# Two stacked transformers on one core: setup redone, buffer pools and the seam between the stacks rearranged

## The chip, the cores and the metric

The kernel runs on one core of a Trainium2 chip. The metric is the device time of one execution, in microseconds (us). "PE" is TensorE's matmul, "PEld" its weight load, DVE is VectorE, ACT is ScalarE, POOL is GpSimd, and SP is SyncE, which mostly issues DMAs. ACT and POOL issue DMAs too. Everything is float32.

## The reference

The input x has 2 sequences of 2048 tokens with 256 features. Six rows of conditioning (a shift, a gain and a gate for each of two stacks) come from c, one vector for each sequence.

```python
mod = (silu(c) @ wmod).reshape(2, 6, 1, 256)
sa, ca, ga, sb, cb, gb = (mod[:, i] for i in range(6))
ga, gb = away_from_zero(ga), away_from_zero(gb)       # |g| is at least 0.25
h = layernorm(x) * (1 + ca) + sa
x = x + ga * stack1(h)
h = layernorm(x) * (1 + cb) + sb
x = x + gb * stack2(h)

def stack1(out):                                       # 3 layers, 16 heads of 16
    for l in range(3):
        q, k, v = out @ Wq + bq, out @ Wk + bk, out @ Wv + bv
        Q, K = favor(q, omega), favor(k, omega)        # [exp(u - h), exp(-u - h)], u = q @ omega
        a = causal_linear_attention(Q, K, v)           # running sums of K v and of K
        h = layer_norm(out + a @ Wo + bo) * g1 + b1
        out = layer_norm(h + relu(h @ W1 + bf1) @ W2 + bf2) * g2 + b2
    return out

def stack2(x):                                         # 2 layers, 8 heads of 64
    for l in range(2):
        q, k, v = split(shift_token(x) @ wqkv)
        q, k = rotary_xpos(l2norm(q) * qs, l2norm(k) * ks)
        x = x + window_attention(q, k, v, 128) @ wo    # own and previous window of 128
        a, g = split((norm(shift_token(x)) * lg + lb) @ w1 + b1)   # 682 features each
        x = x + (a * gelu(g)) @ w2 + b2
    return x
```

## The kernel before

**Setup.** A pool `pro` holds what only the setup uses. `wmod` comes on two queues (L232), then all weights of the three layers of stack 1 on SP's queue (L251; the first Wq on ACT's). silu(c) is made by one ACT and three DVE operations (`sg`, L258 to L261). Twenty-four small matmuls make the six conditioning rows (`pm`, L300; `mod`, L307). Rows that must lie along the free axis on all 128 partitions (gains and biases of the norms) are kept in `brow`: `spread` widens columns on DVE (`wide`, L279), transposes them on PE (`rowtp`, L287) and copies them on ACT (L288). `omt` (L330 to L337) holds the matrices of the random features.

**Stack 1** works on 16 blocks of 256 tokens: 8 positions n of each sequence b. `favor_block(b, n)` loads x, normalizes (`normed`: statistics L354 and L355, `rs` L357 and L358, `dn` L361), turns to features on partitions (`turned`: four PE transposes `ntp` L371, ACT scale and shift L375), makes the residual on POOL (`scaled`: `res`, L382 to L385), and runs three layers, `favor_layer`. A layer: `pq` L414, `xs` L425, `pv` L430, the features `pu` L453 and `ft` L463, the running sum of K and its product with Q (`z`, POOL L484 and L485), `tk` L489, the scores `sc` L500 masked into `att` L506, `su` L520, the denominators `den` L548, the numerators `nd` L559 and L572, `po` L602, a norm, and the MLP (`pf` L624, `fr` on ACT L632, `acc` L635, the sum `s` L647), and a norm. A carried state `st` (L593) joins a block to the next of its sequence.

Four blocks are in work at once. `planned(jobs, 4)` lets each block run from one `yield` to the next and writes their steps into one order for PE by the times that the yields give: a step's own time, the time until its next can start, and a key ("attention", "mlp") that one block holds at a time. PE works this list in order. The other engines are ordered by a scheduler, and each works its own list in order too.

At the end of a block, `x1` = x + gate x output is written to DRAM (`xmid`, L685), normalized again, turned to `hm` and written to `hmid` (L690).

**Stack 2** loads the entry streams `s` from `hmid` (L724) with 16 loads at its start; a column between two 512-token streams is copied on POOL (L713), the first set to zero (L711), for the shift by one token. Each of its 2 layers has 32 attention tiles of 128 tokens and then an MLP over blocks of 512 tokens. The order on PE, DVE, ACT and POOL is written by hand: the table `WHEN` gives every step of a tile (names such as "q", "tp", "s0", "po") a time in units of one tile, about 14 us, and the steps of all tiles are sorted by tile number plus that time. A tile has `pqkv` L790 (q, k, v, a bank of PSUM each), cos and sin products (`qk` L802, `raw` L813, `rot` POOL L832, the sum L854), the l2 norm (`sq` L824, `ss` L842, L859), transposes `tp` L869, the copies `qT` and `kT`, `sim` L886, the softmax (`mx` L918, `ex` L926, `sum` L936, `pm` on POOL L941), transposes `ptp` L953 and copies `pT` L961, `av` L979, `po` L998, then the sum and norm of the MLP's entry (`mean` and `var` L1021). The MLP has `pg` and `pa` L1135, gelu L1143, the product L1144, `acc` L1173. A layer's MLP weights come by `load_mlp` and `load_w2`.

PSUM has 8 banks of 512 floats for each partition. Stack 1 divides them by tag: "mm" 3, "sc" 4, "acc" 1, in one pool. Stack 2 takes all 8 as one ring, `bank(name)`: each request gets the bank that was asked for longest ago, and waits until its last reader is done. SBUF is laid out by pools; where a pool is closed, what is opened later may lie on its place, and its first writer then waits for the last user of that place.

Of the kernel before, what the change touches and what calls it, by code (L numbers as in the profile page):

```python
# [8 lines left out]
F32 = mybir.dt.float32  # L9
# [5 lines left out]
P = 128  # L15
# [24 lines left out]
def block_kernel(ctx: ExitStack, tc: tile.TileContext, t: dict, out: bass.AP):  # L40
# [19 lines left out]
    nc.sync.dma_start(cst, t["consts"])  # L60
# [11 lines left out]
    mhalf = const.tile([P, 16], F32, name="mhalf")  # L72
    nc.gpsimd.memset(mhalf, -0.5)
    mod = const.tile([P, 6, KT, B], F32, name="mod")
    omt = const.tile([P, LA, 2, 4, 2, 8], F32, name="omt")
    bvb = const.tile([P, LA, D], F32, name="bvb")
    nc.gpsimd.dma_start(bvb, t["bv"].partition_broadcast(P))
# [54 lines left out]
    }  # L132
    FEED = 0.32
# [75 lines left out]
    attn_w, mlp_w = {}, {}  # L209


    with ExitStack() as c1:
        wp = c1.enter_context(tc.tile_pool(name="wA", bufs=1))
        psum = c1.enter_context(tc.tile_pool(name="psA", bufs=1, space=PSUM))
        brow = wp.tile([P, NROW, D], F32, name="brow")
        hp = c1.enter_context(tc.tile_pool(name="hA", bufs=3))
        work = c1.enter_context(tc.tile_pool(name="workA", bufs=2))

# [7 lines left out]
        def mm_tile(name):  # L226
            return psum.tile([P, TB], F32, tag="mm", name=name, bufs=3)

        with tc.tile_pool(name="pro", bufs=1) as pro:
            wmod = pro.tile([P, KT, 6 * D], F32, name="wmod")  # L230
            for kt in range(KT):
                (nc.scalar if kt else nc.sync).dma_start(wmod[:, kt, :], t["wmod"][kt * P : (kt + 1) * P, :])  # L232
            early = {b: load_x(b, 0) for b in range(B)}
            om_rep = pro.tile([P, LA, 8], F32, name="om_rep")
            for h in range(8):
                nc.gpsimd.dma_start(om_rep[16 * h : 16 * h + 16], t["omega"].rearrange("l d m -> d l m"))
            W = {}
            for l in range(LA):
                pool = shared if l < 2 else wp
                wa = pool.tile([P, ROOM], F32, tag=f"wa{l}", name=f"wa{l}")  # L240
                wb = pool.tile([P, ROOM], F32, tag=f"wb{l}", name=f"wb{l}")
                for room, at, name, kts, width in (
                    (wa, KT * DFF, "Wq", KT, D),
                    (wa, KT * DFF + KT * D, "Wk", KT, D),
                    (wb, NF * D, "Wv", KT, D),
                    (wb, NF * D + KT * D, "Wo", KT, D),
                    (wa, 0, "W1", KT, DFF),
                    (wb, 0, "W2", NF, D),
                ):
                    w = room[:, at : at + kts * width].rearrange("p (k n) -> p k n", k=kts)  # L250
                    (nc.scalar if (name, l) == ("Wq", 0) else nc.sync).dma_start(  # L251
                        w, t[name][l].rearrange("(k p) n -> p k n", p=P)
                    )
                    W[name, l] = w

            cv = vec[:, V_C : V_C + KT * B]
            sg = pro.tile([P, KT * B], F32, name="sg")
            nc.scalar.activation(sg, cv, AF.Exp, scale=-1.0)  # L258
            nc.vector.tensor_scalar(sg, sg, 1.0, None, ALU.add)
            nc.vector.reciprocal(sg, sg)  # L260
            nc.vector.tensor_tensor(sg, sg, cv, ALU.mult)  # L261

            cols = pro.tile([P, NROW, KT], F32, name="cols")

            def col(i, *parts):
                op = parts[2] if len(parts) > 2 else ALU.add
                if len(parts) == 1:
                    nc.vector.tensor_copy(cols[:, i, :], parts[0])
                else:
                    nc.vector.tensor_tensor(cols[:, i, :], parts[0], parts[1], op)  # L270

            def va(l, name):
                o = V_A + l * VA_N + VA[name]
                return vec[:, o : o + KT]

            def spread(lo, hi):
                for i in range(lo, hi, 2):
                    wide = pro.tile([P, 2 * KT, P], F32, tag="wide", name="wide", bufs=2)
                    nc.vector.tensor_copy(  # L279
                        wide,  # L280
                        cols[:, i : i + 2, :].rearrange("p a k -> p (a k)").unsqueeze(2).to_broadcast(
                            [P, 2 * KT, P]
                        ),
                    )
                    tp = mm_tile("rowtp").rearrange("p (a c) -> p a c", c=P)
                    for k in range(2 * KT):
                        nc.tensor.transpose(tp[:, k, :], wide[:, k, :], ident)  # L287
                    nc.scalar.copy(brow[:, i : i + 2, :].rearrange("p a (k c) -> p (a k) c", c=P), tp)  # L288

            for l in range(LA):  # L290
                col(R_G1 + l, va(l, "g1"))
                col(R_B1 + l, va(l, "b1"), va(l, "bf2"))
            for l in range(LA - 1):
                col(R_G2 + l, va(l, "g2"))
                col(R_B2 + l, va(l, "b2"), va(l + 1, "bo"))
            spread(0, R_G0)
            pm = mm_tile("pm")
            for m in range(6 * KT):
                for kt in range(KT):
                    nc.tensor.matmul(  # L300
                        pm[:, m * B : (m + 1) * B],
                        wmod[:, kt, m * P : (m + 1) * P],
                        sg[:, kt * B : (kt + 1) * B],
                        start=(kt == 0),
                        stop=(kt == KT - 1),
                    )
            nc.vector.tensor_copy(mod.rearrange("p a k b -> p (a k b)"), pm[:, : 6 * KT * B])  # L307
            for i in (1, 4):
                nc.vector.tensor_scalar(mod[:, i], mod[:, i], 1.0, None, ALU.add)
            for i in (2, 5):  # L310
                sgn = pro.tile([P, KT, B], F32, name=f"sgn{i}")
                nc.vector.tensor_scalar(sgn, mod[:, i], 0.0, 2.0, ALU.is_ge, ALU.mult)
                nc.vector.tensor_scalar(sgn, sgn, -1.0, None, ALU.add)
                neg = pro.tile([P, KT, B], F32, name=f"neg{i}")
# [4 lines left out]
            for b in range(B):  # L319
                col(R_G0 + b, mod[:, 1, :, b])  # L320
                col(R_B0 + b, mod[:, 0, :, b], va(0, "bo"))
                col(R_GE + b, va(LA - 1, "g2"), mod[:, 2, :, b], ALU.mult)
                col(R_BE + b, va(LA - 1, "b2"), mod[:, 2, :, b], ALU.mult)
            spread(R_G0, NROW)


            for hf in range(2):
                own, other = slice(64 * hf, 64 * hf + 64), slice(64 - 64 * hf, 128 - 64 * hf)
                for l in range(LA):
                    nc.vector.tensor_tensor(  # L330
                        omt[own, l, hf].rearrange("p h s m -> p (h s) m"),
                        om_rep[own, l, :].unsqueeze(1).to_broadcast([64, 8, 8]),
                        hm2[own, 8 * hf : 8 * hf + 8].unsqueeze(2).to_broadcast([64, 8, 8]),
                        ALU.mult,
                    )
                    nc.vector.tensor_scalar(omt[own, l, hf], omt[own, l, hf], 0.5, None, ALU.mult)
                    nc.vector.tensor_scalar(  # L337
                        omt[other, l, hf].rearrange("p h s m -> p (h s m)"),
                        nhalf[other, 64 - 64 * hf : 128 - 64 * hf],
                        0.25,  # L340
                        None,
                        ALU.mult,
                    )

        rp = c1.enter_context(tc.tile_pool(name="rA", bufs=2))
        fp = c1.enter_context(tc.tile_pool(name="featA", bufs=2))
        sp = c1.enter_context(tc.tile_pool(name="smallA", bufs=2))

        def normed(src):

            mv = sp.tile([P, NCA, 2], F32, tag="mv", name="mv")
            for c in range(NCA):
                bs = sp.tile([P, 6], F32, tag="bs", name="bs")
                nc.vector.bn_stats(bs, src[:, c, :])  # L354
                nc.vector.bn_aggr(mv[:, c, :], bs)  # L355
            rs = sp.tile([P, NCA], F32, tag="rs", name="rs")
            nc.scalar.activation(rs, mv[:, :, 1], AF.Ln, bias=eps_t)  # L357
            nc.scalar.activation(rs, rs, AF.Exp, scale=-0.5)  # L358
            dn = work.tile([P, NCA, D], F32, tag="dn", name="dn", bufs=3)
# [33 lines left out]
        nc.vector.tensor_reduce(par, hmask.rearrange("p (i q) -> p q i", q=2), AX.X, ALU.add)  # L393
# [5 lines left out]
        turn = [0]  # L399

        def favor_layer(b, n, l, h, hres):
# [45 lines left out]
            yield 5.2, 0.6, "attention"  # L447
            feat = []
# [44 lines left out]
            def scores(c):  # L493

                cs = slice(c * P, (c + 1) * P)
                scs = [psum.tile([P, KT, 2, P], F32, tag="sc", name="sc", bufs=4) for _ in range(4)]
# [121 lines left out]
            acc = psum.tile([P, NCA, D], F32, tag="acc", name="acc", bufs=1)  # L618
            fr = {}
            for f in range(NF + 1):  # L620
                if f < NF:
                    pf = psum.tile([P, TA], F32, tag="sc", name="pf", bufs=4)
# [8 lines left out]
                    fr[f] = fp.tile([P, TA], F32, tag="fr", name="fr", bufs=3)  # L631
# [16 lines left out]
            dn = normed(s)  # L648
# [9 lines left out]
        def next_weights():  # L658

            late.append(0)  # L660
            if len(late) == B:
                attn_w[0] = load_attn(0)
                mlp_w[0] = load_mlp(0)
# [663 lines left out]
```

## Time and profile before

| | |
|---|---|
| median of 3 runs | 3002.98 us (3001.48 to 3004.59) |
| profiled execution | 3000.0 us, span 2998.2 us |
| mean granted PE clock | 0.992 |
| PE | 2914.3 us busy (97% of the span), 19356 instructions |
| PEld | 2132.3 us (71%) |
| DVE | 1686.0 us (56%), 4194 instructions |
| ACT | 1344.5 us (45%), 3269 instructions |
| POOL | 1065.1 us (36%), 937 instructions |
| DMA | 57.10 MB, mean 19 GB/s |

The span is the profiled execution from its first to its last instruction, and the time of that execution has 1.8 us more. Busy times leave out the issuing of DMAs and waiting. In a chain of waits each line is a start, a length, and the work or wait that the next piece followed; "issue" is time in which the engine waited for nothing that the profile shows. PE's clock is the share of its full speed that the chip granted. A matmul shows as two records, a transpose as one.

### The profile page before, as it was taken

The page shows a single profiled execution, that of the slowest core. Times are in us where ns is not written, and L with a number is a line of the kernel's source. Part 1 is how long each engine was busy: PE and PEld are TensorE (multiplying, and loading weights), DVE is VectorE, ACT ScalarE, POOL GpSimd, SP SyncE. Part 2 cuts the span into 40 slices and gives each one's busy share as a digit, 9 for nine tenths or more (in the row PEclk, how much of TensorE's full clock was granted, in tenths as well). Part 3 has the DMA queues.
Part 4 walks back from the last instruction along what each step waited for, and adds up shares of the span by engine and source line. Part 5 has one row for each costly group of instructions (what it writes and reads, how often), then busy time and mean ns, then how long its engine had stood idle before and what let it go on. Part 6 is the DMA issues. An engine that isn't in the chain of part 4 may idle for free.

```text
span 2998.2 us, 49213 instructions
## 1 busy us (share of the span) xinstructions
PE 2914.3 (97%) x19356; PEld 2132.3 (71%) x19356; DVE 1686.0 (56%) x4194; ACT 1344.5 (45%) x3269; POOL 1065.1 (36%) x937
## 2 busy tenths in 40 slices
PE   6999999999999999999996999999999999999999
PEld 5888888888888888888873777776444777776444
DVE  5555565555565555655543777774224777775222
ACT  2333343334343334434333676665113766766211
POOL 2222233222332223322233666663002666664000
PEclk9999999999999999999997999999999999999999
DMA  5000010000100000001012000001000000000011
GB/s 184 1 1 1 1 36 22 1 1 1 36 22 1 1 1 29 29 1 43 15 42 77 1 1 1 1 1 58 0 0 10 20 1 1 2 1 8 28 43 35
DMA packets 37399, 57.10 MB, mean 19 GB/s; under 512 B 3720, under 2 KB 28720, under 8 KB 36656
## 3 DMA queue, kind: packets, MB, share of 16 engines
q1 hardware_dynamic: 36288, 52.37, 5.3%
q8 instruction: 153, 2.51, 0.3%
q0 software_dynamic: 464, 0.54, 0.1%
q10 hardware_dynamic: 416, 1.05, 0.1%
q14 instruction: 78, 0.64, 0.1%
HBM read 41.37 MB, written 12.58 MB: 18 GB/s over the span
## 4 chain that ended last, share of the span: by engine, by line
PE 88%; DVE 4%; ACT 3%; POOL 2%; DMA 1%; issue 1%; SPq 1%; DVEq 0%; ACTq 0%; POOLq 0%
PE acc L635 11%; PE pf L624 10%; PE pqkv L790 10%; PE pg L1135 5%; PE pq L414 5%; PE acc L1173 5%; PE pa L1135 4%; PE av L979 4%; PE sim L886 3%; PE ptp L953 3%; PE po L998 3%; PE sc L500 3%; PE nd L572 3%; PE pu L453 3%; PE pv L430 3%; PE po L602 3%
## 5 line engine op out<-in xcount | busy, mean ns | idle before, releaser
L635 PE MATMUL acc<-wb,fr 128*128 128x256 f32 x1536 | 397.3, 381 | 5.4 <-ACT fr L632 5.1
L624 PE MATMUL pf<-h,wa 128*128 128x256 f32 x1536 | 400.2, 384 | 1.1 <-ACT h L375 0.7
L632 ACT ACTIVATE fr<-pf,vec 128x256 f32<-128x256 f32 x384 | 180.6, 471 | 425.8 <-PE pf L624 425.0
L790 PE MATMUL pqkv<-wqkv,s 128*128 128x512 f32 x768 | 358.0, 602 | 8.3 <-issue 8.3
L506 DVE TENSOR_TENSOR att<-sc,cst 128x512 f32<-128x512 f32 x384 | 238.3, 683 | 157.6 <-PE sc L500 157.6
L635 PEld LDWEIGHTS acc<-wb,fr 128*128 128x128 f32 x1536 | 287.8, 190 | 52.0 <-ACT fr L632 8.6
L384 POOL TENSOR_TENSOR res<-dn,brow 128x512 f32<-128x512 f32 x112 | 144.7, 1292 | 485.2 <-DVE dn L361 473.5
L624 PEld LDWEIGHTS pf<-h,wa 128*128 128x128 f32 x1536 | 275.8, 190 | 55.7 <-issue 19.5
L941 POOL TENSOR_TENSOR pm<-pm,sum 128x1024 f32<-128x1024 f32 (+1 forms) x128 | 235.7, 1842 | 178.9 <-DVE sum L936 178.9
L926 ACT ACTIVATE pm<-pm,mx 128x256 f32<-128x256 f32 (+1 forms) x512 | 249.4, 489 | 58.9 <-DVE mx L918 58.7
L790 PEld LDWEIGHTS pqkv<-wqkv,s 128*128 128x128 f32 x768 | 138.0, 193 | 135.9 <-issue 134.0
L832 POOL TENSOR_TENSOR rot<-raw,rsn_wo 128x512 f32<-128x512 f32 x128 | 160.5, 1275 | 183.5 <-ACT raw L813 183.5
L1144 DVE SCALAR_TENSOR_TENSOR ge<-pa,vec,ge 128x512 f32<-128x512 f32 x80 | 60.1, 751 | 281.9 <-PE pa L1135 230.6
L1143 ACT ACTIVATE ge<-pg,vec 128x512 f32<-128x512 f32 x96 | 65.8, 686 | 314.9 <-PE pg L1135 314.9
L426 ACT ACTIVATE xs<-xs 64x512 f32<-64x512 f32 x192 | 120.6, 628 | 152.3 <-DVE xs L425 142.8
L1135 PE MATMUL pg<-s,w 128*128 128x512 f32 (+1 forms) x384 | 182.2, 597 | 0.0
L414 PE MATMUL pq<-h,wa 128*128 128x256 f32 x768 | 175.4, 382 | 0.0
L425 DVE TENSOR_TENSOR xs<-pq,vec 64x512 f32<-64x512 f32 x192 | 132.2, 688 | 76.5 <-PE pq L414 72.7
L1173 PE MATMUL acc<-ge,w 128*128 128x512 f32 (+1 forms) x384 | 168.8, 600 | 0.0
L414 PEld LDWEIGHTS pq<-h,wa 128*128 128x128 f32 x768 | 146.1, 191 | 21.1 <-issue 1.4
L854 POOL TENSOR_TENSOR qk<-qk,rot 128x1024 f32<-128x1024 f32 x64 | 151.5, 2367 | 0.5
L1135 PE MATMUL pa<-s,w 128*128 128x512 f32 x320 | 150.4, 592 | 0.0
(163 smaller groups left out, 5361.8 us busy)
## 6 DMA issues: line engine op xcount, KB each, us to landing
xin<-in_x_dram SPq DMA_DIRECT2D x32, 256.0 KB, 2.8
x<-res SPq DMA_DIRECT2D x16, 256.0 KB, 2.1
h<-hm SPq DMA_DIRECT2D x16, 256.0 KB, 2.4
s<-h SPq DMA_DIRECT2D x16, 256.0 KB, 5.4
xl<-x SPq DMA_DIRECT2D x8, 512.0 KB, 4.2
out_dram<-res SPq DMA_DIRECT2D x8, 512.0 KB, 3.2
w<-in_w_dram SPq DMA_DIRECT2D x6, 640.0 KB, 4.0
wa<-in_W_dram SPq DMA_DIRECT2D x3, 1024.0 KB, 8.9
```

The costliest lines, as they stand in the source:

```text
L414: nc.tensor.matmul(pq[:, g, :], W[wn, l][:, kt, g * P : (g + 1) * P], h[:, kt, :], start=(kt == 0), stop=(kt == KT - 1),)
L506: nc.vector.tensor_tensor(am, scs[i].rearrange("p g q c -> p (g q) c"), caus.unsqueeze(1).to_broadcast([P, 2 * KT, P]), ALU.mult,)
L624: nc.tensor.matmul(pf, W["W1", l][:, kt, f * P : (f + 1) * P], h1[:, kt, :], start=(kt == 0), stop=(kt == KT - 1),)
L632: nc.scalar.activation(fr[f], pf, AF.Relu, bias=v("bf1", f))
L635: nc.tensor.matmul(acc[:, c, :], fr[f - 1][:, c * P : (c + 1) * P], W["W2", l][:, f - 1, :], start=(f == 1 and c == 0), stop=(f == NF), sk ...
L790: nc.tensor.matmul(pq, s[:, kt * TB + c * P : kt * TB + (c + 1) * P], wqkv[:, kt, i * INNER : (i + 1) * INNER], start=(kt == 0), stop=(kt ...
L832: nc.gpsimd.tensor_tensor(rot[:, :, :, lo : lo + 32], got["raw"][:, :, :, hi : hi + 32], rsn[:, ti, :, lo : lo + 32].unsqueeze(2).to_broad ...
L854: nc.gpsimd.tensor_tensor(got["qk"], got["qk"], got["rot"], ALU.add)
L926: nc.scalar.activation(pm[:, hd, :], pm[:, hd, :], AF.Exp, bias=of("mx", hg)[:, hd : hd + 1], accum_out=of("sum", hg)[:, hd : hd + 1],)
L941: nc.gpsimd.tensor_tensor(pm, pm, of("sum", hg).unsqueeze(2).to_broadcast([P, 4, kw]), ALU.mult)
L1135: nc.tensor.matmul(pt[:m, :], w1[:, kt, off : off + m], hb[:, kt * TB : (kt + 1) * TB], start=(kt == 0), stop=(kt == KT - 1),)
L1173: nc.tensor.matmul(acc[m], w2[rs_, f, m * P : (m + 1) * P], g[rs_, :], start=(f == 0), stop=(f == NFH - 1),)
```

## The change

In the **setup**, the pool `pro` goes. `wmod` and the scratch `stage` take the places that layer 2's weights fill later. The constants come in two parts, the identity first; `wmod` comes in two parts, the first two rows of conditioning on ACT's queue and the other four on SP's behind W1 of layer 0. The random features' `om_rep` are POOL's first DMAs. `spread` transposes the columns themselves (8, 20 and 8 rows), copies them on ACT, stores them to DRAM (`rows_out`) and loads them on all partitions, both by POOL's queue. `first_norm` writes the order up to the first block's norm by hand, and `rest_of_setup` is one more job of `planned`: the other four rows of conditioning, the random features of layers 1 and 2, the third `spread`, and then the loads of layer 2's weights. Of the first blocks the residual is made only after the first projections (`hres` may be a function).

The **pools** are laid in another order. Stack 1's PSUM becomes three pools. Stack 2's PSUM becomes two rings, of 3 banks (`pqkv`, `mean`, `var`, `acc`, `ntp`) and of 5 (all others). In SBUF, the values `v` and sums `ss` get a pool of their own, and the streams two, of 4 and 12.

At the **seam**, the last block of each sequence ends with its last layer's norm, written into the room `last`. Its `x1`, second norm and transposes become steps of stack 2 in tiles 3 to 6 (`last_sum`, `last_stats`, `last_dev`, `last_norm`, `last_tokens`), and the transposes go straight to the stream. Entry streams are loaded by `load_stream`, the first at once, the others at tile time 1.1; the column between two streams is loaded too. The table `FIRST` moves q, k and v of the first tiles ahead, `turn_mask` (the mask `win_r`) becomes a step at 2.0, and both layers load their MLP's weights at tile 8.

```diff
+    FIRST = [
+        {"v": -1.1},
+        {"q": -0.58, "k": -0.45, "v": -1.59},
+        {"q": -0.97, "k": -0.3, "v": -1.56},
+        {"q": -0.96, "k": -0.18},
+    ]
+    TAKES = {"q": ("cosq", "cq"), "k": ("ck", "cosk"), "v": ("cv",)}
...
-        psum = c1.enter_context(tc.tile_pool(name="psA", bufs=1, space=PSUM))
+        psum_mm, psum_sc, psum_acc = (
+            c1.enter_context(tc.tile_pool(name=f"psA{i}", bufs=1, space=PSUM)) for i in range(3)
+        )
...
+        nc.scalar.dma_start(wmod[:, :, : 2 * D], wmod_in[:, :, : 2 * D])
+        early = {(b, 0): load_x(b, 0) for b in range(B)}
+        nc.sync.dma_start(cst[:, P:], t["consts"][:, P:])
...
+        load_weights(0, "Wq", "Wk", "Wv", "Wo")
+        early[0, 1] = load_x(0, 1)
+        load_weights(0, "W1")
+        nc.sync.dma_start(wmod[:, :, 2 * D :], wmod_in[:, :, 2 * D :])
+        load_weights(0, "W2")
+        load_weights(1, "Wq", "Wk", "Wv", "Wo", "W1", "W2")
...
+        def spread(lo, hi):
+            n = (hi - lo) * KT
+            tp = mm_tile("rowtp")[:n, :P]
+            nc.tensor.transpose(tp, cols[:, lo:hi, :].rearrange("p a k -> p (a k)"), ident)
+            turned_ = turned_cols.pop()[:n]
+            nc.scalar.copy(turned_, tp)
+            nc.gpsimd.dma_start(rows_out[lo * KT : hi * KT], turned_)
+            nc.gpsimd.dma_start(
+                brow[:, lo:hi, :].rearrange("p a d -> p (a d)"),
+                rows_out[lo * KT : hi * KT].rearrange("a c -> (a c)").partition_broadcast(P),
+            )
...
+        def first_norm(normed, turned):
...
+                condition(0, 2, pm)
...
+                dn = normed(early.pop((0, 0)))
+                conditioned(0, 2, pm)
+                h = hp.tile([P, KT, TA], F32, tag="h", name="h0")
+                turned(dn, h, lambda k: mod[:, 1, k, 0:1], lambda k: mod[:, 0, k, 0:1])
...
+                spread(R_G0, R_GE)
+                spread(0, R_G0)
+                omega_rows(0)
...
+        def rest_of_setup():
+            yield 0.0, 8.0, "mlp"
+            pm = psum_acc.tile([P, NCA * D], F32, tag="acc", name="pm2", bufs=1)
+            for i in range(2, 6):
+                condition(i, i + 1, pm)
+                yield 1.7, 0.0, "mlp"
+            conditioned(2, 6, pm)
+            for l in range(1, LA):
+                omega_rows(l)
...
+            spread(R_GE, NROW)
+            load_weights(2, "Wq", "Wk", "Wv", "Wo", "W1", "W2")
+            yield 0.2, 0.0
...
             yield 5.2, 0.6, "attention"
+            if callable(hres):
+                hres = hres()
...
-            dn = normed(s)
+            ends = l == LA - 1 and n == S // TA - 1
+            dn = normed(s, last[0][:, b] if ends else None)
...
             if n == S // TA - 1:
                 next_weights()
+                return
...
+            with tc.issue_after(last_first):
+                planned(blocks[:1] + [rest_of_setup()] + blocks[1:], 4)
...
         def bank(name):
-            return psum.tile([P, TB], F32, tag="ps", name=name, bufs=8)
+            k = int(name not in ("pqkv", "mean", "var", "acc", "ntp"))
+            return psums[k].tile([P, TB], F32, tag="ps", name=name, bufs=(3, 5)[k])
...
+        def load_stream(b, n):
+            s = entry[b, n] = stream_tile(f"s_{b}_{n}")
+            own = slice(0, TB if n < NB - 1 else TB - TA)
+            if n == 0:
+                nc.gpsimd.memset(s[:, TB : TB + 1], 0.0)
+            else:
+                nc.sync.dma_start(s[:, TB : TB + 1], hmid[b, n - 1][:, 1, TB - 1 :])
+            for kt in range(KT):
+                nc.sync.dma_start(rows(s)[kt][:, own], hmid[b, n][:, kt, own])
+
+        load_stream(0, 0)
...
-                steps += [(start + i + WHEN[k], l, i, f) for k, f in ops.items()]
-                if l > 0 and i == NCH:
+                when = dict(WHEN)
+                for k, shift in FIRST[i].items() if l == 0 and i < len(FIRST) else ():
+                    for k2 in (k, *TAKES[k]):
+                        when[k2] += shift
+                steps += [(start + i + when[k], l, i, f) for k, f in ops.items()]
+                if i == 2 * NCH:
                     steps.append((start + i, l, i, partial(load_mlp_late, l)))
+            if l == 0:
+                for b in range(B):
+                    steps += [
+                        (start + 3 + 2 * b + w, l, b, partial(f, b, *a))
+                        for w, f, *a in (
+                            (0.0, last_sum, 0), (0.46, last_sum, 1), (0.96, last_sum, 2), (1.2, last_stats),
+                            (1.21, last_dev), (1.35, last_norm), (1.61, last_tokens),
+                        )
+                    ]
+                steps.append((start + 2.0, l, 0, turn_mask))
+                blocks = [(b, n) for b in range(B) for n in range(NB)][1:]
+                steps += [(start + 1.1, l, i, partial(load_stream, *blk)) for i, blk in enumerate(blocks)]
```

## The prediction

> **What bounds the kernel now.** I read the page first: PE is busy 2914.3 of 2998.2 us and holds 88% of the chain that ended last. A change that leaves PE's work alone can win only where PE stands still or runs below full clock: 84 us of idle time in all. So I asked for windows. Columns: stretch, length, busy (instructions) of PE, PEld, DVE, ACT, POOL, then PE's clock, DMA share, GB/s.
>
> ```profile
> 0.00:20.00 20.00, 10.34 (x48) 9.86 (x49) 5.72 (x36) 4.42 (x7) 5.71 (x16) 1.00 0.94 315
> 20.00:40.00 20.00, 9.69 (x45) 8.67 (x45) 8.56 (x42) 5.07 (x12) 6.84 (x7) 0.87 1.02 346
> 40.00:60.00 20.00, 15.57 (x90) 11.11 (x91) 13.23 (x26) 7.22 (x15) 9.04 (x8) 0.79 0.10 26
> ...
> 1580.00:1600.00 20.00, 3.88 (x16) 2.53 (x16) 4.07 (x14) 3.38 (x9) 3.15 (x5) 0.61 0.35 115
> 1600.00:1620.00 20.00, 13.96 (x41) 6.82 (x40) 6.14 (x8) 4.34 (x8) 5.78 (x10) 0.71 0.48 169
> 1620.00:1640.00 20.00, 15.92 (x70) 8.08 (x69) 13.22 (x49) 9.54 (x32) 11.78 (x8) 0.91 0.01 1
> 1640.00:1660.00 20.00, 19.22 (x140) 14.48 (x140) 14.15 (x40) 14.53 (x46) 13.71 (x11) 1.00 0.00 1
> 1660.00:2000.00 340.00, 339.04 (x2519) 249.55 (x2519) 260.03 (x774) 236.10 (x689) 227.69 (x177) 1.00 0.00 1
> ```
>
> The two places are plain: the first 60 us (PE idle 24.4, DMA full for 40) and the seam (idle 27.0 in 1580 to 1660, clock 0.61 to 0.91). The tile loop behind has no idle time (339.04 of 340). Next the chain of waits, at the start:
>
> ```profile
> 26.99 12.37 DMA xin<-in_x_dram
> ...
> 39.38 0.75 DVE bs L354 x2
> ...
> 45.44 0.90 PE ntp L371 x3
> 46.34 4.50 PE pq L414 x16
> ...
> 60.75 1.06 PE den L548 x4
> ```
>
> PE's order puts the transposes of four blocks ahead of the first projection, and the x of the third and fourth comes behind all weights: 46 us pass before stack 1 begins. The seam, same view:
>
> ```profile
> 1581.97 0.76 DVE s L647 x2
> ...
> 1589.78 1.15 PE ntp L371 x4
> ...
> 1592.00 4.10 DMA h<-hm
> ...
> 1598.46 5.50 DMA s<-h
> ...
> 1615.36 3.33 PE pqkv L790 x4
> ...
> 1647.36 1.93 PE sim L886 x16
> ```
>
> The last block's sum, norm, transposes, store and loads run one after another, then the tile pipeline fills with nothing to cover its chain; `pqkv` takes 3.33 for four records, against 1.72 in the loop (the same view at 1658.57).
>
> **Setup.** First pq: vec is there at 4.1 (DVE's first copy); silu is one ACT 0.20 and three DVE ops of 0.1, so 5.0. The first part of wmod, 512 KB, is there about then (768 KB took 4.5 on this queue). Of the 24 pm matmuls, 10.24 together, 0.427 each, 8 stay in front: 8.5. x(0,0) goes up to third on SP; statistics 0.75, rs 0.5, dn 0.75, four transposes 0.45, two h0 on ACT 1.0: first pq at 10.4 instead of 46.3. This is an estimate; its DMAs are the loose part.
>
> What follows is POOL's. Before, brow was made by 36 rowtp records (8.38 us of PE) and ACT copies. Now two round trips through DRAM stand in POOL's order, and behind them four res operations (1.27 each, 5.1), a state (0.73) and z (1.27): 7.3 with the small copy. PE's den waits for z, and behind den stand nd and all that PE does next. The rows start at 11. Bounds of the round trip: h<-hm landed in 2.4 (median) in an idle stretch, and 1.8 MB at the 350 GB/s of the second window takes 5.1: 7.5. On the full queues of the start om_rep (1.5 KB) took 7.6 and bvb (384 KB) 8.0: with the 5.1, 20.7. So brow lands at 18.5 to 32. I take 25, nearer the middle since 8.7 MB of other loads share the engines to about 25. Then z is there at 32.5 (26 to 39.5). PE's own way to den: 14.4 as before (46.34 to 60.75), plus 5.1 for 12 pm matmuls laid between, less what those hide: 28 (27 to 30). So den is at 32.5 (27.5 to 39.5), 28.2 earlier than 60.75. Behind den are now four pm matmuls 1.7, one block's transposes 0.45 and a rowtp 0.1: 26.0. Blocks come less ready than before, 1.5: **gain 24.5** (14 to 30, the low end with the rest of wmod late too). Wq, Wk and Wv shared between ACT's and SP's queues land by 10, since 2.7 MB had landed by then before; late by 2 is 2 lost. Layer-2 weights now go behind setup on SP: 3 MB at 350 GB/s is 9 us, and the first block needs them after two layers, over 50 us later: nothing; without that cover, 9. Layer-1 omega steps on DVE, 0.2 each, hide beside PE's scores.
>
> [...]
>
> **Seam.** Work at full clock in 1580 to 1660: busy 3.88 + 13.96 + 15.92 + 19.22 = 53.0, less what the low clock added, 3.88x0.39 + 13.96x0.29 + 15.92x0.09 = 7.0: 46.0. After, tiles 0 to 3 load as soon as the last attention is done; the built order shows the first stream's load waiting for nothing later, and PE's list continues with six pqkv groups at the last acc. Six times 1.72 is 10.3. q and k are done at 3.4, then cos 0.70, raw 0.59, rot 2.5, add 2.35, norm 1.23 make 10.8 to 11.1: tp of tile 0 waits 0.85. Down the list, with the loop's durations: v 0.4, tp of tile 1 1.5, its p copies 0.8, sims 0.4, po of tile 0 3.3. Sum 7.3 idle. So 80 becomes 46.0 + 7.3 = 53.3: 26.7, plus 1.3 in 1540 to 1580 where acc waited for an fr behind the norm steps that leave ACT's order: **gain 28.0** (20, if the fill's stalls double, to 33, if most of them vanish). The last blocks' x1, norm and transposes become steps of tiles 3 to 6: six POOL sums of 1.27 are 7.6, where POOL is busy 227.69 of 340 and has 4.6 free in each tile of 14; two ntp groups of 0.45 stay PE work. Cost 0; without that cover 7.6. The first MLP's weights at tile 8 go past SP's empty queue (DMA share 0.00) with 24 tiles left: 0, or 4 at most.
>
> On the clock: the trace shows it at 0.61, 0.71, 0.91 over 60 us. With the gaps down to 3.3 I count none of the 7.0 left. [...]
>
> **Tile loop and MLPs.** PSUM becomes rings of 3 and 5 banks. The order of instructions in the loop stays; new waits come. In a steady tile (timeline):
>
> ```profile
> 1787.53 2.00 PE L886 MATMUL sim<-kT,qT 64*128 64x256 f32 x16
> 1787.63 0.69 DVE L961 COPY pT<-ptp 128x512 f32<-128x512 f32 x1
> ```
>
> The second bank of s1 now waits for this copy, which ends at 1788.32; its first matmul there is the sixth of eight, at about 1788.73. Slack 0.4: cost 0, above 0 only if DVE comes later. Bounds over 64 tiles: fewer semaphores, -1; slack gone by 0.2, +12. The MLP's new waits have 3 to 5 us of cover (5.15 of PE each f step; gelu 0.69). At the two entries into the MLPs a sim waits for the gelu of the pg just issued, covered by only one pa (1.72), while ACT also loads a table (1.28): 0 to 4 each, I take 1.5: **loss 3**. Pools laid differently in SBUF: no instruction, 0.
>
> **Sum**, on the profiled run (3000.0; span 2998.2): 3000.0 - 24.5 - 28.0 + 3 = 2950.5. The runs' median is 3.0 above it: 2953.
>
> **Rivals.** A: the setup gives back its gain. brow lands at 32 or later and pm2 waits for the rest of wmod; setup 14 instead of 24.5: 2963. For: DMA share 0.94 and 1.02, tiny transfers 7.6. Against: the DMA stands idle from 32 on.
> B: the seam starts earlier, but the fill keeps its stalls and its low clock: only 1581.97 to the first pqkv at 1599.2 goes, 17.2 instead of 28.0: 2964. For: q-to-tp stays one long chain over ACT, POOL, DVE. Against: six groups in front cover it.
> C, slower: the split banks tax every tile. If the pT copies come late, PE stands at sim and the order, written by hand, passes it on. 64 tiles at 1 us are 64, less the 52.5 - 3 gained: 3017. It decides from 0.8 us a tile. For: the copy ends only 0.4 before. Against: this slack, and DVE is busy 76% in the loop.
> D: the change doesn't do what it says at the seam: the first stream's buffer lies over one that lives to the end of the last MLP, or its load lands late, so that the chain stays. Seam 0: 2981. For: one SBUF for both. Against: the load has 14 us of MLP over it, and took 5.5.
>
> **Chances.** Forecast 0.58, A 0.13, B 0.12, D 0.10, C 0.07. A difference under 0.2%, 6 us, can't be told from none. All but C are faster by more; C is slower, with 0.01 of it near its break-even. Range: from both gains at their best (30 + 33, no loss: 2940, and 3 for a spread of the runs) to D (2981, and 2): 2937 to 2983.
>
> **What would show it.** In the profile after: first pq near 10; den waiting for z at 28 to 33 (near 40: A); idle in the first 80 us down from 25.8 to about 11; in the 54 us after the last acc under 8 idle and clock 1.00 (B: below 0.8); no gap before the first pqkv (D: 8 or more); sim without a releaser in the tile loop, 14.0 a tile (C: DVE pT); 1 to 2 us before the first MLP steps. If idle of PE falls by less than 35 in all, or the tile loop's share of busy time falls below 0.99, the prediction is wrong.

## The result: 2984.4 us, a third of the gain that was forecast

The changed kernel takes 2984.42 us (median of 6 runs, 2984.01 to 2985.58) against 3002.26 for the kernel before in the same comparison: ratio 0.9942, 95% interval 0.9929 to 0.9955, 17.8 us faster. The forecast was 2953, with a range from 2937 to 2983. Its profiled run has a span of 2982.6, 15.6 less than before.

To see where the time went, I set the same operation of both traces side by side: the n-th relu `fr` of stack 1 (384 in each), the n-th `raw` copy of stack 2 (two a tile, 128), the n-th gelu of the MLPs. The order of these is nearly the same in both kernels, so the difference of their starts is what has been gained by then.

| up to | operation | before | changed | gained so far |
|---|---|---|---|---|
| the 17th relu | fr 16 | 158.76 | 136.45 | 22.3 |
| shortly before the end of stack 1 | fr 352 | 1500.65 | 1478.31 | 22.3 |
| tile 10 of stack 2 | raw 20 | 1741.71 | 1706.90 | 34.8 |
| tile 30 | raw 60 | 2021.29 | 1994.07 | 27.2 |
| tile 0 of layer 1 | raw 64 | 2281.43 | 2254.97 | 26.5 |
| tile 30 of layer 1 | raw 124 | 2706.24 | 2689.22 | 17.0 |
| last MLP | gelu 88 | 2952.50 | 2936.22 | 16.3 |

So the setup gave 22.3, the seam 12.5, and each steady tile of the loop took back 0.38 (27.2 against 34.8 over 20 tiles): 18 us over the two layers.

The windows of the changed kernel, columns as above. The first three answer to the three of before; the seam now lies some 20 us earlier:

```profile
0.00:20.00 20.00, 13.76 (x53) 11.47 (x54) 11.36 (x51) 6.83 (x17) 9.22 (x22) 1.00 0.95 326
20.00:40.00 20.00, 17.82 (x169) 14.42 (x168) 12.58 (x45) 4.90 (x9) 9.93 (x9) 0.76 0.97 337
40.00:60.00 20.00, 17.55 (x115) 13.23 (x115) 14.80 (x31) 8.33 (x18) 8.98 (x9) 0.98 0.37 119
...
1580.00:1600.00 20.00, 13.74 (x87) 10.27 (x87) 14.41 (x41) 11.55 (x43) 12.65 (x11) 0.91 0.00 1
1600.00:1620.00 20.00, 17.09 (x135) 12.65 (x133) 18.50 (x49) 13.42 (x39) 14.79 (x13) 1.00 0.04 14
1620.00:1640.00 20.00, 19.25 (x142) 14.47 (x143) 14.30 (x47) 10.21 (x30) 14.15 (x11) 0.91 0.00 1
1640.00:2000.00 360.00, 349.36 (x2544) 256.08 (x2542) 269.35 (x789) 243.42 (x712) 232.25 (x181) 1.00 0.02 6
```

The last line is the surprise: PE was busy 339.04 of 340 in the tile loop before, and now stands still for 10.6 of 360. The prediction named two signs that it is wrong, an idle time of PE that falls by less than 35 in all and a loop that is busy for less than 0.99. Both are there: 13.1 (83.9 to 70.8) and 0.97. The chain of waits in the setup, against that of before:

```profile
16.80 6.69 DMA brow<-rows_out
...
23.64 2.95 POOL res L455 x2
...
29.86 1.24 POOL z L559
...
31.14 2.08 PE den L622 x4
```

brow lands at 23.5, POOL works off the residuals, and den starts at 31.1 instead of 60.8. The forecast had 25 and 32.5. Here the steps hold.

Now a steady tile of the loop in the changed kernel (timeline):

```profile
1768.62 2.00 PE L1015 MATMUL sim<-kT,qT 64*128 64x256 f32 x16
1768.73 0.69 DVE L1090 COPY pT<-ptp 128x512 f32<-128x512 f32 x1
...
1770.31 0.57 ACT L1090 COPY pT<-ptp 128x512 f32<-128x512 f32 x1
...
1770.93 1.97 PE L1108 MATMUL av<-pT,v 128*64 128x128 f32 x32 [0.31 <-ACT pT L1090]
```

The sims run through beside DVE's copy, as was forecast. But av, right behind them, now waits for ACT's copy pT, which ends at 1770.88. Before, av did not wait there (timeline of the kernel before, same place in a tile):

```profile
1789.21 0.57 ACT L961 COPY pT<-ptp 128x512 f32<-128x512 f32 x1
...
1789.45 0.77 PE L979 MATMUL av<-pT,v 128*64 128x128 f32 x10
```

av started 0.33 before ACT's copy ended: its first matmuls read the pT that DVE had copied, only the later ones need ACT's. It also overlapped the last sims by 0.08 (they ended at 1789.53); with the 0.31 that makes up, within rounding, the 0.38 of a tile. In the built order of the changed kernel the first matmul of av waits for ACT's pT, because av is given the PSUM bank that this copy reads. Four sims hold the other four banks of the ring of 5. (The description ahead of the prediction says that a request gets the bank asked for longest ago. By that the second bank of s1 would have had to wait for ACT's copy, and the sims ran through. The waits fit banks that come free in the order of their last readers: in `WHEN`, DVE's copy "pb1" stands at 2.595 and ACT's "pa1" at 2.674.)

### The profile page after: what moved, and what is told of

Same layout as the page of the kernel before. It is cut to its first block, busy times and chain, and to the rows that moved or that the text cites. A ratio compares the mean times of both kernels' runs of the same rounds, so it can differ in the third digit from the quotient of the medians.

```text
span 2982.6 us, 49076 instructions
## 1 busy us (share of the span) xinstructions
PE 2911.8 (98%) x19323; PEld 2131.9 (71%) x19323; DVE 1694.9 (57%) x4186; ACT 1340.6 (45%) x3263; POOL 1068.7 (36%) x937
## 4 chain that ended last, share of the span: by engine, by line
PE 83%; ACT 7%; DVE 5%; issue 2%; POOL 2%; DMA 1%; ACTq 0%; DVEq 0%; POOLq 0%
PE acc L709 10%; PE pf L698 10%; PE pqkv L919 10%; PE pg L1264 5%; PE pq L486 5%; PE acc L1302 5%; PE pa L1264 4%; PE av L1108 4%; PE po L1127 3%; PE nd L646 3%; PE sc L574 3%; PE pu L527 3%; PE po L676 3%; PE pv L502 3%; ACT sq L953 2%
## 5 line engine op out<-in xcount | busy, mean ns | idle before, releaser
L1127 PEld LDWEIGHTS po<-oT,rsn_wo 128*128 128x128 f32 x1024 | 125.3, 193 | 37.0 <-issue 15.3
## 6 DMA issues: line engine op xcount, KB each, us to landing
wa<-in_W_dram SPq DMA_DIRECT2D x3, 1024.0 KB, 11.4
```

The lines of the kernel that those rows point to most:

```text
L1127: nc.tensor.matmul(po[:, m, :], wo[:, k, m * P : (m + 1) * P], got["oT"][:, k, :], start=(k == 0), stop=(k == INNER // P - 1),)
```

## The experiments

The theory after the comparison had three parts: the ring of 5 banks costs 0.38 a tile and more at the seam; the setup is bounded by brow's round trip through POOL's order; and the rest of the seam's shortfall is stalls of the fill, some of them on DVE operations that stand beside POOL's. The rival for each was that something else in the change (the order of the SBUF pools, the steps `last_*`) takes the time. Gains "at the seam" below are between fr 352 and raw 20, as in the table.

**One ring of 8 banks** (e1_ring8).

```diff
...
-            k = int(name not in ("pqkv", "mean", "var", "acc", "ntp"))
-            return psums[k].tile([P, TB], F32, tag="ps", name=name, bufs=(3, 5)[k])
+            return psum.tile([P, TB], F32, tag="ps", name=name, bufs=8)
```

> The changed kernel with one ring of 8 PSUM banks in stack 2 instead of rings of 3 and 5; nothing else. Theory (rings): in the changed kernel a tile lasts 14.40 us instead of 14.02, because av gets the bank whose last reader is the ACT copy pT of the same tile (0.31 idle before av in every tile), and in two tiles of the seam the bank of a sim that DVE still reads (2.08 and 2.02). With 8 banks these waits go: 0.38 x 57 tiles = 21.7, the two gaps 4.1, and about 1.7 each for the half clock behind them: 2984.4 - 29 = 2955, range 2952 to 2963. Rival (the tax comes from the other order of SBUF pools or from steps at the seam): 2984 within 3, tile still 14.40. Second rival (the single ring makes the first projections wait for banks of the last MLP): tile 14.02, but a gap of some us before the first pqkv, 2960 or more.

Measured: 2964.47 (2957.92 to 2966.56), ratio to before 0.9871 (0.9856 to 0.9886), 20 us faster than the changed kernel. From tile 10 to tile 30 the loop loses 0.01 instead of 7.6; the line that answers to the last one of the windows above:

```profile
1640.00:2000.00 360.00, 358.00 (x2631) 262.16 (x2628) 278.36 (x831) 250.57 (x737) 241.22 (x188) 1.00 0.02 6
```

The tax is the rings'. The median lies 1.5 above the range that the theory gave: the seam gained 3.0 (12.5 to 15.5) where 7.5 was expected. The two gaps of 2 us before av went, but other small gaps grew (1.37 before po, 1.00 before the first pqkv), this run's setup gained 1.3 less, and each entry into an MLP lost 1.6.

**The rings alone, in the kernel before** (e2_before_rings). The same edit, the other way round, with nothing else of the change.

> The kernel before with PSUM rings of 3 and 5 banks in stack 2 instead of one of 8; nothing else. Theory (rings): every tile of both layers is 0.38 longer, 0.38 x 62 = 23.6: 3026, range 3020 to 3030, with 0.31 idle before av. Rival: 3002 within 3.

Measured: 3024.44, ratio 1.0072 (1.0055 to 1.0089): 22.3 slower, inside the theory's range. The line of the tile (timeline):

```profile
1781.66 1.53 PE L982 MATMUL av<-pT,v 128*64 128x128 f32 x24 [0.31 <-ACT pT L964]
```

The same wait with the same 0.31, in a kernel that has nothing else of the change. In its trace the tiles of the loops take 18.6 more, 0.38 for each of 20 steady ones, as in the changed kernel. With both runs this is settled.

**FIRST empty** (e3_no_first).

```diff
-    FIRST = [
-        {"v": -1.1},
...
+    FIRST = []
```

> The changed kernel with the table FIRST empty, so that the projections of tiles 0 to 3 stand where the tile table puts them. Theory (the projections drawn ahead are what covers the first chain from q to tp): the gap before tp of tile 0 goes from 0.9 back to 6 and that of tile 1 from 1.3 to 3, 6.8 more idle, and the clock falls to half behind it, up to 7: 2991 to 2998. Rival (the early load alone brings the seam's gain, the fill is bound by later waits such as the one before po): 2984 within 3.

Measured: 2988.95, ratio 0.9957 (0.9942 to 0.9972), 4.5 slower than the changed kernel, between the theory's range and the rival's. The gaps before tp were 6.01 and 2.94 again, as expected; but of the gap of 4.74 before po only 0.79 was left (timeline):

```profile
1572.31 1.94 PE L993 MATMUL tp<-cst,qk 128*128 128x128 f32 x8 [6.01 <-DVE qk L983]
...
1599.13 1.05 PE L1122 MATMUL po<-oT,rsn_wo 128*128 128x128 f32 x7 [0.79 <-DVE oT L1114]
```

So drawing the projections ahead had moved more than half of the wait from one place to another. What holds that place became the next question.

**The bound of ss with two inputs** (e4_ss_two_inputs). In the fill of the changed kernel (timeline, DVE, POOL, PE), tile 2's ss stands in front of what po of tile 0 needs:

```profile
1587.47 2.35 POOL L983 TENSOR_TENSOR qk<-qk,rot 128x1024 f32<-128x1024 f32 x1
...
1587.49 2.36 DVE L972 TENSOR_SCALAR ss<-ss 128x16 f32<-128x16 f32 x1
...
1593.33 3.46 PE L1127 MATMUL po<-oT,rsn_wo 128*128 128x128 f32 x16 [4.74 <-DVE oT L1119]
```

An operation of 16 columns lasts 2.36, as long as the POOL sum beside it. In the loop, where it starts 0.14 before the POOL operation beside it ends, it takes 0.17 (at 1771.38). The expectation counts the two long ones, 1.39 and 2.36, to tiles 0 and 1; in the order of the ss they are those of tiles 1 and 2.

```diff
-                nc.vector.tensor_scalar(ss, ss, 1e-24, None, ALU.max)
+                nc.vector.tensor_tensor(ss, ss, floor, ALU.max)
```

> The changed kernel with the lower bound of ss taken by a DVE operation of two inputs (tensor_tensor max against a constant tile) instead of tensor_scalar. In the changed kernel this 128x16 operation lasts 0.17 in the loop, but 1.39 and 2.36 in tiles 0 and 1, where it ends within 0.05 of the end of POOL's qk sum running beside it; the gap of 4.74 before the first full po hangs on it. Theory (this form of DVE operation stands still while a POOL tensor_tensor runs, one of two tensor inputs does not): ss 0.2 everywhere, the gap before po 2.4 shorter, tile 0's sims read 1.2 earlier: 2981, range 2978 to 2983. Rival (DVE waits there for something else, or the two-input form is held too): 2984 within 2.

Measured: 2984.64, ratio 0.9944 (0.9929 to 0.9959): nothing. The two-input form lasted 1.40 and 2.37 in the same places. So the form chosen was held as well, which left both the theory in another form and the rival open.

**ss in PSUM** (e6_ss_psum, on the ring of 8).

```diff
-                ss = got["ss"] = vp_.tile([P, 2 * NH], F32, tag="ss", name="ss", bufs=2)
+                got["rn"] = bank("rn")
+                ss = got["ss"] = got["rn"][:, 2 * NH : 4 * NH]
...
-                rn = got["rn"] = bank("rn")[:, : 2 * NH]
+                rn = got["rn"] = got["rn"][:, : 2 * NH]
```

> The kernel of e1_ring8, with ss (the sums of squares) in the PSUM bank of rn instead of SBUF; nothing else. The DVE operation that bounds ss lasted 1.39 and 2.36 in tiles 0 and 1 beside a POOL operation, with one or with two SBUF inputs. Theory (DVE and POOL share a way to SBUF, and a DVE operation that needs it stands until POOL's operation ends): reading and writing PSUM alone it takes 0.2 everywhere, and the gap of 4.7 before po falls to about 2.4: 2.3 better, 2 more if the half clock behind that gap goes: 2959 to 2963. Rival (DVE waits there for a semaphore or for sq's data): the operation keeps 2.36, 2964.

Measured: 2955.65 (2955.35 to 2957.16), ratio 0.9846 (0.9833 to 0.9860), faster than the theory's range. The same places in the fill:

```profile
1586.96 2.36 POOL L981 TENSOR_TENSOR qk<-qk,rot 128x1024 f32<-128x1024 f32 x1
...
1586.99 0.18 DVE L970 TENSOR_SCALAR rn<-rn 128x16 f32<-128x16 f32 x1
...
1591.22 1.07 PE L1125 MATMUL po<-oT,rsn_wo 128*128 128x128 f32 x5 [3.13 <-DVE oT L1117]
```

The same operation at the same time as the same POOL sum takes 0.18 when it touches PSUM alone. That this operation is held beside POOL's when it works on SBUF is shown by this and by the run before: one input or two in SBUF, held (2.36 and 2.37); none, free (0.18). It doesn't hold for every DVE operation on SBUF: in the changed kernel the statistics `bs<-s` (128x256, SBUF to SBUF) took 0.41 beside a POOL sum (two from 207.67 on, 0.74 together) and 0.42 without one (two from 204.79 on, 0.74 as well). Why the one is held and the other not, and whether the two engines share a way to SBUF as the theory put it, no trace here shows.

The trace of before already had such rows, in its setup (timeline):

```profile
29.82 0.74 DVE L361 TENSOR_SCALAR dn<-xin,mv,rs 128x256 f32<-128x256 f32 x2
...
31.85 2.35 DVE L361 TENSOR_SCALAR dn<-xin,mv,rs 128x256 f32<-128x256 f32 x2 [0.80 <-ACT rs L358]
...
32.80 1.25 POOL L384 TENSOR_TENSOR res<-dn,brow 128x512 f32<-128x512 f32 x1
```

The same two operations took 0.74 with POOL idle and 2.35 beside POOL's work, so the price could have been read before the prediction.

The seam gained 23.2 instead of 15.5, 7.7 more, of which 1.6 before po, 1.2 before tp, 0.9 before the next po and 2.0 already in the last MLPs of stack 1, which the edit does not touch; the other 2.0 go with the clock in the 15 us around po (0.77 against 0.89). In the last MLPs, and at the entries of the MLPs (1.6 each), the two runs differ by the granted clock (0.66 against 0.83 in 1485 to 1495; 0.83 against 1.00 behind 2010 and 2000), which I don't put down to the edit. PE's idle time says what is left without the clock: from the last relu of stack 1 to raw 20 it is 27.0 in the kernel before, 14.3 in the changed one, 12.3 with the ring of 8 and 8.1 here. So 4.2 of the 8.8 between the two medians is waiting that went; one of the four runs of the ring of 8, at 2957.92, comes within 2.3 of this median.

**FIRST empty with ss in PSUM** (e10_ss_psum_no_first).

> The kernel of e6_ss_psum with the table FIRST empty; nothing else. With ss in SBUF the drawn-ahead projections gained 3.4 at tile 8, since what they took from tp (6.1) came back before po (4.9) where ss stood behind a POOL operation. Theory (the two are tied: with ss no longer held, drawing ahead keeps more of it): 5 to 7 worse than e6_ss_psum, 2961 to 2963. Rival (the fill is bound by the softmax chain of tile 1 either way): 2957 to 2959.

Measured: 2964.14, ratio 0.9877 (0.9863 to 0.9890), 8.5 slower than with FIRST and 1.1 above the theory's range; the seam gained 12.8 instead of 23.2. **FIRST empty with the ring of 8** and ss in SBUF (e8_ring8_no_first):

> The kernel of e1_ring8 with the table FIRST empty. With the rings of 3 and 5 this cost 4.5: 6.8 more idle before tp, 4.4 less before po. Theory (drawing ahead only moves the fill's stalls from tp to po; the net is 2 to 5): 2967 to 2970. Rival (with free banks the drawn-ahead projections bring their full 6.8 and the clock): 2971 to 2978.

Measured: 2965.11, ratio 0.9878 (0.9864 to 0.9891), 0.6 from the ring's own 2964.47 and below both ranges, with a seam of 11.7 against 15.5. So in these traces drawing ahead was worth 3.8 at the seam with ss held and 10.5 with ss free. Part of that is clock; in idle time over the stretch named above it is 1.7 (14.1 to 12.3) and 7.0 (15.1 to 8.1), and 3.9 in the changed kernel (18.3 to 14.3). The two are tied, and the single test of FIRST in the changed kernel told half of it.

**The order of the pools** (e7_pools_as_before). On the ring of 8, stack 1 and stack 2 open their SBUF pools in the order of before (weights, h and work first; streams and weights first).

> The kernel of e1_ring8, with the SBUF pools of both stacks in the order of the kernel before (in stack 1 weights, h and work first; in stack 2 streams, weights, then work); nothing else. In the built order the load of the first stream then waits for the last acc of stack 1, not for the last attention. Theory (the order of the pools is what lets the first projections start at the last acc): a gap before the first pqkv of two issues 0.8 and a landing of 2.4 to 5.5, so 3 to 6, and half clock behind it, up to 3: 2968 to 2974. Rival (the load was late anyway, or other streams' loads wait more): 2964 or over 2976.

Measured: 2965.27, ratio 0.9877 (0.9863 to 0.9890): no difference that can be told. The wait is there (timeline):

```profile
1563.67 3.32 PE L916 MATMUL pqkv<-wqkv,s 128*128 128x512 f32 x4 [3.19 <-DMA s<-h]
```

It is 2.2 more than with the new order (1.00), but a later gap before po shrank from 1.37 to 0.47, and PE's idle time from the last relu of stack 1 to raw 20 is 13.7 instead of 12.3. The seam gained 15.6, no less than with the ring alone, because the last MLPs of stack 1, ahead of the wait, ran at a higher clock here (0.83 against 0.66 in 1485 to 1495); from the last relu to raw 20 this run is 1.8 slower. The pools' order does what it says; it is worth 1 to 2 us there, less than the 3 to 6 expected, and the medians can't show it.

**The residuals behind z** (e5_res_late). On the ring of 8:

```diff
-            if callable(hres):
-                hres = hres()
             feat = []
...
             nc.gpsimd.tensor_tensor(z, qf, z, ALU.mult)
+            if callable(hres):
+                hres = hres()
```

> The kernel of e1_ring8 (one ring of 8), with the residual of the first blocks made on POOL after z instead of before it; nothing else. In the changed kernel den of the first block waited 2.06 us for z, which stood behind four res operations that wait for brow (landed at 23.5). Theory (the round trip through DRAM reaches PE only through POOL's order): the gap before den goes, den at 29 instead of 31, setup 2 better, and up to 5 more if the half clock from 30 on follows that gap: 2957 to 2963 against 2964.5 for e1_ring8. Rival (the wait passes to po or to the next norm, which need res too): 2964.

Measured: 2955.82 (2951.31 to 2963.96), ratio 0.9849 (0.9833 to 0.9864). The scheduler still put three of the residual operations ahead of z; den waited 1.85 instead of 3.86 in the run with the ring alone. The setup gained 23.9 instead of 21.0. The trace is that of a run of 2963.2, against 2966.56 for the ring's: with the setup it explains 3 of the 8.7 us between the medians. The runs of the two kernels overlap (the ring's reach from 2957.92 to 2966.56), and what makes these five spread over 12.7 us is not shown.

**All together** (e9_together): ring of 8, ss in PSUM, and z forced ahead of every residual and of the state's sum. The edit of the last part:

```diff
+            z_made = nc.gpsimd.tensor_tensor(z, qf, z, ALU.mult)
+            if callable(hres):
+                with tc.issue_after(z_made.ins):
+                    hres = hres()
...
+            with tc.issue_after(z_made.ins):
+                nc.gpsimd.tensor_tensor(state[b, l], states[1], sm[:, 1], ALU.add)
...
-            if n > 0:
+            if n > 1:
                 hres = hres()
```

> The kernel of e6_ss_psum (one ring of 8, ss in PSUM) with POOL's order changed in setup: z stands ahead of every residual that needs brow (those of the first four blocks are made after it), and the state's sum behind z; nothing else. e5_res_late moved only two of four residuals, and den still waited 1.85. Theory (brow's round trip reaches PE only through z's place in POOL's order): z at about 27, no gap before den (4.2 in e6_ss_psum), setup 4 better: 2950 to 2953 against 2955.7. Rival (the wait passes to po or to the next norm, since brow lands no earlier): 2955.

Measured: 2953.62 (2953.20 to 2957.26), ratio 0.9841 (0.9828 to 0.9854), the lowest median, 31 us under the changed kernel. From 2955.65 without the new order of z it can't be told (the intervals overlap). The gap before den is gone, but most of it is back later (timelines, DVE and PE):

```profile
48.15 4.51 DVE L432 TENSOR_SCALAR dn<-xin,mv,rs 128x256 f32<-128x256 f32 x2 [2.27 <-POOL res L455]
...
51.48 0.45 PE L442 MATMUL ntp<-cst,dn 128*128 128x128 f32 x1 [5.66 <-DVE dn L432]
```

The setup gained 23.0, against 21.1 in the trace without the new order and 22.8 in another run with the old one. Theory and rival each had a part: the wait on POOL's order was real, and behind it stands the norm, whose dn (two operations, 4.51 together, beside the residuals on POOL) lasts as ss did; most dn of this trace take 0.41 each. An order that keeps this dn away from POOL's residuals was not tried.

## Why the prediction was wrong

- **Setup: right in mechanism and nearly in size.** First pq at 11.4 (10.4 forecast), brow at 23.5 (25), den waiting 2.1 for z (4.5), gain 22.3 (24.5). The missing 2.2 is behind den: den starts 29.6 earlier than before (28.2 forecast), and 7.3 of that is lost by the 17th relu, where the sum had 3.75. PE's clock was 0.50 from 30.4 to 40.7, which the sum left out. In runs with the same setup the gain varied between 21.0 and 22.8, with the wait before den between 2.1 and 4.2. One reading against rival A was wrong: the DMA of before doesn't stand idle "from 32 on", its share is 0.86 in 35 to 40. A failed all the same, by brow's landing.
- **Tile loop: the step that failed first.** "Slack 0.4: cost 0" was worked out for one place, the second bank of s1, and it held there. But a ring of 5 gives every request a new predecessor, not only the sims: the request right behind, av, got the bank of an ACT copy that ends 0.33 after av used to start. That row stood in the same timeline, a few lines below the two that were quoted. Going through all of a tile's requests would have given 0.33 a tile, about 20 us, instead of 0. The measured cost is 0.38 a tile, 18 us here and the same in the loops of the kernel before with the rings alone. Rival C had the right family and the wrong place, with a price of 1 a tile.
- **Seam: 28.0 forecast, 12.5 measured.** The start is as forecast: the gap before the first pqkv fell from 8.28 to none, that before tp of tile 0 to 0.89 (0.85 forecast), tile 1's to 1.28 (1.5). Of the 15.5 that are missing, 7.0 is idle time: 14.3 from the last relu to raw 20, where the forecast left 7.3. The ring makes 4.1 of it, by two gaps of 2 us before av in the tiles in which the bank it gets is one that a sim still holds for DVE. At po of tile 0 (4.74 instead of 3.3) "with the loop's durations" failed: ss has 0.17 in the loop, where the hand-written order lets it start as POOL's operation ends, and 1.39 and 2.36 in the fill, where the order is the same but the times are not. With ss in PSUM po waits 3.13, and with the ring of 8 as well the idle time is 8.1, near the forecast.
- **The clock at the seam: 7.7 of the 15.5.** "I count none of the 7.0 left" was wrong by 5.2. PE's busy time from the last relu to raw 20 fell by 1.8 only (134.8 to 133.0), with a clock of 0.91 in 1580 to 1600, 1620 to 1640 and 1640 to 1660: behind the gap of 4.74 before po and those of 2.08 and 2.02 before av it was 0.50 in 1593.7 to 1597.1, 1621.0 to 1624.4 and 1655.1 to 1658.5, which makes 5.1 of the 5.2. Another 2.5 went in the last MLPs, which the sum left out: PE is busy 77.1 there instead of 74.5, at 0.96 instead of 1.00, behind a gap of 2.86 where the trace of before had one of 2.94. Why the clock fell in one and not in the other stays open. The last 0.8 is the 1.3 that the sum had in 1540 to 1580, of which 0.5 came.
- **Entries into the MLPs: a loss of 3 forecast, none to be seen** (0.76 each from tile 30 on, which is the tax of two tiles). No wait for a gelu stands there; the loss of 1.6 that some runs with the ring of 8 have at each entry is clock (0.83 in 2010 to 2020 of the ring's run).
- **Cases.** The kernel is faster, so A, B and D had the sign; none had this sum. B's price for the seam (17.2) plus a tile tax of a third of C's comes close, and such a sum of two half rivals was not among the cases. Its time, 2984, lies just outside a range that ended at D.

The missing 33 us (49.5 forecast, 16.3 by the last MLP) are 2.2 of the setup, 15.5 of the seam and 15.5 of loop and MLP entries. That the combination of the runs measures 2953.6, the forecast's own number, is chance: it comes from a ring of 8 and an ss in PSUM, which this change doesn't have, and from 22.7 at the seam, not 28.0.

## What to carry to other kernels

Where a ring of buffers is made shorter, list every request of one period with the last reader of the buffer it will get, and compare that reader's end with the start that the request has now: a single slack of the wrong sign in a loop of 64 outweighs the repair of a seam. A loop's durations can't be carried to its fill where another engine's operations lie beside them at other times (ss: 0.17 in the loop, 2.36 in the fill). And test parts of a change in pairs: drawing work ahead saved 1.7 us of idle time at the seam while a later wait stood, and 7.0 once it was gone.

## What the runs showed of the hardware that was not expected

A DVE operation of 16 columns, with one or two tensor inputs in SBUF, lasted 2.36 and 2.37 us beside a POOL sum of 2.35 and ended with it; in PSUM it took 0.18. DVE's statistics of 256 columns, in SBUF too, took 0.41 beside POOL and 0.42 without. Granted clock fell for some us behind gaps of 2 to 5 us in some places (4.74 before po: 0.50 in 1593.7 to 1597.1 of the changed kernel; 2.02 before av: 0.50 in 1655.1 to 1658.5) and not in others with the same gap (2.94 before ntp: 1.00 in 1508 to 1513 of the kernel before, 0.66 in the same stretch of the kernel before with the rings alone, whose code there is the same; 2.86: 0.50 in 1485 to 1490 of the changed one), so a few us of difference between two runs need not come from the edit.
